# A transformer block on one core: where weight stores are issued, how weights are asked for ahead, and how buffers for gathered rows are cut

## The chip, the core and the metric

The kernel runs on one core of a Trainium2 chip. A core has five engines with queues of their own: TensorE (PE in the profile) multiplies matrices, VectorE (DVE) and ScalarE (ACT) do elementwise work and read the matmul results from PSUM, GpSimd (POOL) does elementwise work on SBUF and issues indirect copies, and SyncE (SP) only issues copies. Copies (DMAs) can be issued from the queues of SP, ScalarE and GpSimd; a queue runs its instructions in order, so an instruction that waits holds up all behind it. The metric is the device time of one execution in microseconds. Before the change it is 1752.19 us (median of three runs, 1750.74 to 1757.38).

## What is computed

A cross-attention step adds to `x` (4 x 512 x 512) a mixture of its own normalised rows; then comes a transformer layer with 16 causal heads of width 128 and a mixture of 16 experts, of which each token uses 6, beside a shared expert. Cut to what matters:

```
# cross-attention, per batch
x = x + layernorm(x) @ softmax((ctx Wq^T + bq) (ctx Wk^T + bk)^T)
# layer on h0 = layernorm(x)
h = rmsnorm(h0) * ln1;  q, k, v = h wq, h wk, h wv          # 16 heads of 128
x2 = h0 + softmax(causal(q k^T / sqrt(128))) v @ wo
t = rmsnorm(x2) * ln2
cw = top 6 of softmax(t gate^T), normalised
routed = sum over the 6 experts e: cw_e * (silu(t eg_e^T) * (t eu_e^T)) @ ed_e^T
shared = (silu(t sg^T) * (t su^T)) @ sd^T
out = x + x2 + routed + shared
```

All of it is in float32. The kernel keeps that precision by splitting each float32 operand into two float16 halves, high and low.

## The kernel before

**Split and product.** `split` (L72 to 74) turns a float32 tile into halves: ScalarE writes the high one (L73), VectorE the low one (L74). `mm3` (L80 to 88) multiplies two split operands with three matmuls per term (lines L83, L86, L87 of the profile). Transposes are made by DMAs on SP's queue (`flip`, L91).

**Order.** The program is written out straight and is handed to a planner that orders the instructions of each engine from a simulated timeline (`schedule_with_timeline_sim=True`) and sets the semaphores. `after(a, b)` only says that `a` comes behind `b` on the same engine's queue; `pin` keeps an instruction in program order. A tile from a pool with `bufs=n` can be filled again only when every reader of the tile n before it is through, DMAs that store it included.

**Stage 1, cross-attention (`xattn(b)`).** Batch 0 runs at the start, batch 1 soon behind it, batches 2 and 3 are spread over the attention loop. For each of four token tiles `t` the result `xv` (the new residual, L337) is stored to DRAM, `x1_d` (L339): from SP's queue for batch 0, from GpSimd's for the others. Then come the statistics on VectorE, a power on GpSimd (L347, which makes a reciprocal root), the normalised row `hd` or `x2` on GpSimd (L354), for batches 2 and 3 its store `hid_d` (L356), the split of `hh` and its transpose into `hT`.

**Stage 2, attention (the loop at L799, one head per step `n`, 64 in all).** A step multiplies `hT` with a head's `wqk` (`queries`) and every second step with `wv` (`values`), forms scores and softmax (`scores`, with the transpose of `pn` into `pt`), weighs the values of the head one step back (`attend`), and, when a group of two heads is through, multiplies with `wo` (`project`, L719 to 724) one step after its second head was weighed. A group is run for two batches in a row with the same weights.

`fetch` (L416 to 453) supplies weights. The first time a weight is wanted it is loaded as float32 into a staging tile `st` (L442, GpSimd's queue but for one; two staging tiles, shared with other loads of the loop), split, and the halves are stored to DRAM (`wqk_d`, `wv_d`, `wo_d`; L448, GpSimd's queue but for `wqk0`). Later the halves are loaded from there (L425, on ScalarE's queue); with `behind` given, that load is issued ahead of use, behind the instruction named. `wqk` and `wv` are asked for two steps ahead (L817 to 821), `wo` right after the group's second head was weighed, one step ahead of `project`:

```python
            attend(b, h)
            if h % HG == HG - 1:
                ready.append((b, h // HG))
                wo_of(b, h // HG, zz["ao"])
```

In steps 8 to 23 `pad_rows` (L498 to 502) copies 384 KB of zeros per step into the buffer of routed rows, from GpSimd's queue, each behind the weight store named `zz["pad"]`. `rest_step` (L541 to 549) reads `x1_d` back, adds, and stores `r_d`, all on GpSimd.

**Stage 3, shared expert and experts.** `gate_up` makes the shared expert's hidden activations in six chunks `ic`, three to a tile of `hs`, two such tiles (L741, L783, L875); `shared_down` (L768 to 781) multiplies them. Each of 16 experts runs in two halves (`gate_up_rows`, then `down_rows` with the store of `yt`, L1148). In the last experts rows of results are gathered back, 96 gathers of 128 rows in all (`gather`, L1194, GpSimd), and added with their weights on VectorE (L1203). Each gathered block takes a place in a ring: two tiles of three places, of the same tag as `hs`; an addition is put into the program once more than four gathered blocks are waiting (`lookahead`, `place`, `add`). After the experts the shared expert of the last batch runs, with the last gathers in tiles of `xin`.

Of the kernel before, what the change touches and what calls it, by code (L numbers as in the profile page):

```python
# [9 lines left out]
F16 = mybir.dt.float16  # L10
F32 = mybir.dt.float32
# [6 lines left out]
P = 128  # L18
# [37 lines left out]
def xattn_moe_block_kernel(ctx: ExitStack, tc: tile.TileContext, x, xT, ctxT, wqkx, bqk, ln1, ln2,  # L56
# [147 lines left out]
    def xattn(b):  # L204
# [127 lines left out]
        for t in range(NT):  # L332
            ps = bank("w", f"xm{b}_{t}")
            tl = slice(t * P, (t + 1) * P)
            xv = xt[:, t, :]
            zz["xm", b, t] = mm3(ps, [(lnp[:, c, tl], lnp[:, C + c, tl], ptp[:, c], ptp[:, C + c]) for c in range(C)])
            nc.vector.scalar_tensor_tensor(xv, ps, rs[:, t:t + 1], xv, ALU.mult, ALU.add)  # L337
            q = nc.gpsimd if b else nc.sync
            q.dma_start(x1_d[b][:, t, :], xv)  # L339
            st = asm.tile([P, 6], F32, name="st")  # L340
            nc.vector.bn_stats(st, xv)
            mv = asm.tile([P, 2], F32, name="mv")
            nc.vector.bn_aggr(mv, st)
            r2 = asm.tile([P, 2], F32, name="r2")
            nc.vector.tensor_scalar(r2[:, 0:1], mv[:, 1:2], 1e-5, None, ALU.add)
            nc.vector.tensor_scalar(r2[:, 1:2], mv[:, 1:2], 1.0 + 1e-6, 1e-11, ALU.mult, ALU.add)
            nc.gpsimd.tensor_tensor(r2, r2, mhalf[:, :2], ALU.pow)  # L347
            hu = tmp("hu", F32)
            nc.vector.scalar_tensor_tensor(hu, xv, mv[:, 0:1], ln1b, ALU.subtract, ALU.mult)
            yield  # L350
            nb = asm.tile([P, 1], F32, name="nb")
            nc.vector.scalar_tensor_tensor(nb, mv[:, 0:1], -1.0, r2[:, 0:1], ALU.mult, ALU.mult)
            hd = x2s[b][:, t] if b < 2 else tmp("hd", F32)
            nc.gpsimd.tensor_scalar(hd, xv, r2[:, 0:1], nb, ALU.mult, ALU.add)  # L354
            if b >= 2:
                q.dma_start(hid_d[b][:, t, :], hd)  # L356
            if stop == "A":
                nc.sync.dma_start(out[b, tl], hd)
            yield
            hh, hi, lo = pair(tmp("hh", F16))  # L360
            zz["hh", b] = split(hi, lo, hu, r2[:, 1:2])[1]
            zz["hT", b] = flip(hT[b][:, :, tl], hh)
            yield

# [51 lines left out]
    def fetch(b, g, pool, tag, n, src, scr, nm, behind=None):  # L416
        if behind and (nm not in seen or nm in soon):
            return
        if held.get(nm, (None,))[0] == (b, g):
            return None if behind else held.pop(nm)[1]  # L420
        w = soon.pop(nm, None)
        if w is None:
            w = pool.tile([P, 2, n], F16, tag=tag, name=f"{nm}_{b}")
            if nm in seen:
                ins = nc.scalar.dma_start(w.rearrange("p a n -> p (a n)"), scr)  # L425
                if behind:
                    after(ins, behind)
        if behind:
            soon[nm] = w
            return  # L430
        if (b, g) in partner:
            held[nm] = partner[b, g], w
        if nm in seen:
            return w
        seen.add(nm)
        first = nm in early_st
        if first:
            st_ = early_st[nm]
        else:
            st_ = stg.tile([P, 1024], F32, tag="st", name=f"{nm}_st")  # L440
            q = nc.sync if nm == "wqk1" else nc.gpsimd
            ins = q.dma_start(st_[:, :n], src)  # L442
            if nm == "wqk1":
                after(ins, zz["hT", 0])
        for j, ins in enumerate(split(w[:, 0], w[:, 1], st_[:, :n], WS)):
            if first:
                after(ins, zz["nb"] if j else zz["calm"][0])
        ins = (nc.sync if nm == "wqk0" else nc.gpsimd).dma_start(scr, w.rearrange("p a n -> p (a n)"))  # L448
        if nm != "wqk0":
            zz["pad"] = ins  # L450
        if nm == "wqk0":
            after(ins, zz["ptp", 0])
        return w

    pieces = []

# [278 lines left out]
    def gate_up(b, hid, tmp):  # L735
        shw = shx["w"]
        hs = []
        for ic in range(6):
            R = P if ic < 5 else SR
            if ic % 3 == 0:  # L740
                hs.append(hid().rearrange("p (i a s) -> p i a s", i=3, a=2))  # L741
            h = hs[-1][:, ic % 3]

            def proj(ps, a):
                o0 = ic * 8 * P + a * C * P
                zz["gu"] = mm3(ps, [(shw[:, 0, o0 + c * P:o0 + (c + 1) * P], shw[:, 1, o0 + c * P:o0 + (c + 1) * P],
                          h2T[b][:, c], h2T[b][:, C + c]) for c in range(C)])
# [20 lines left out]
    def shared_down(b, hs, last=False, tick=lambda src: None):  # L768
        sdw = shx["d"]
        acc = residual(b)  # L770
        for t in range(NT):
            tl = slice(t * P, (t + 1) * P)
            ps = bank("s", f"sy{b}_{t}")
            mm3(ps, [(hs[ic // 3][:, ic % 3, 0, tl], hs[ic // 3][:, ic % 3, 1, tl],
                      sdw[:, 0, ic * D:(ic + 1) * D], sdw[:, 1, ic * D:(ic + 1) * D]) for ic in range(5)], stop=False)
            nc.tensor.matmul(ps, hs[1][:, 2, 0, tl], sdw[:, 0, 5 * D:], start=False, stop=False)
            nc.tensor.matmul(ps, hs[1][:SR, 2, 1, tl], sdw[:SR, 0, 5 * D:], start=False, stop=True)
            zz["acc", b] = nc.vector.scalar_tensor_tensor(acc[:, t], ps, 1.0 / (GS * WS), acc[:, t], ALU.mult, ALU.add)
            if last:
                store(b * NT + t, acc[:, t])  # L780
            tick(acc[0:1, t, 0:1])

    early = gate_up(0, lambda: ht.tile([P, 2 * NT, S], F16, tag="pt", name="hs0").rearrange("p k s -> p (k s)")[:, :6 * S],  # L783
                    lambda: stg.tile([P, 1024], F32, tag="st", name="sg0")[:, :S])

    NH = B * H
# [10 lines left out]
    ready = []  # L797
    bring = iter([j for j in range(2, B) for _ in range(5 * NT + 1)])
    for n in range(NH + LAG + 1):  # L799
        if n < NH:  # L800
            b, h = heads[n]
            if b not in opened:
# [11 lines left out]
            for p in parts:  # L814
                for _ in p:
                    pass
            if n + HG < NH:  # L817
                b, h = heads[n + HG]
                wqk_of(b, h, zz["qk"])
                if h % HG == 0:  # L820
                    wv_of(b, h // HG, zz["qk"])
        m = n - LAG
        if n == NH:
            last_residual(B - 1)
        if n >= NH:
            for ic in range(3 * (n - NH), 3 * (n - NH) + 3):
                hs0 = next(early)
                if scat:
                    pace(hs0[ic // 3][0:1, ic % 3, 0, 0:1])
                    scatter(-(-len(scat) // (6 - ic)))  # L830
        if ready:
            b, g = ready.pop()
# [9 lines left out]
        if 0 <= m < NH:  # L842
            b, h = heads[m]
            attend(b, h)
            if h % HG == HG - 1:
                ready.append((b, h // HG))
                wo_of(b, h // HG, zz["ao"])
        if n in agenda and n < NH:
            b = agenda[n]
            if n + 1 in agenda:  # L850
# [21 lines left out]
    st2 = ctx.enter_context(tc.tile_pool(name="st2", bufs=2, side="right", reuse_waits="tile"))  # L872

    def up(b):
        return gate_up(b, lambda: st2.tile([P, 6 * S], F16, name="hs"), lambda: st2.tile([P, S], F32, name="sgt"))  # L875

    def drip(n, src):
        if scat:
# [34 lines left out]
        return o  # L913

    for ic, hs in zip((4, 5), ups):
        drip(2, hs[1][0:1, ic - 3, 0, 0:1])
    shared_down(1, hs, tick=lambda src: drip(2, src))
    residual(2)
    after(zz["exp"], zz["silu", 1, 1])
# [100 lines left out]
    seat(0)  # L1020
    nxt = ranked_weights(0)
    for ic, hs in enumerate(up(2)):
        drip(3, hs[ic // 3][0:1, ic % 3, 0, 0:1])
        if ic == 4:
            rows_in(0, 0)
            rows_in(0, 1)
# [192 lines left out]
        for _ in range(-(-len(todo) // left)):  # L1219
            gather()  # L1220

    lookahead(lambda: st2.tile([P, 3, D], F32, tag="hs", name="yg"), 3, 4)
    ring["steps"] = 1
    for e in range(E):
        wd = nxt
# [93 lines left out]
```

## Time and profile before

| what | value |
|---|---|
| time, median of three runs | 1752.19 us |
| the profiled execution | 1761.27 us |
| its span, first to last instruction | 1759.5 us |
| mean granted clock of TensorE | 0.993 |
| VectorE, ScalarE, GpSimd busy | 1114.4, 829.5, 459.2 us |
| weight stores on GpSimd (L448) | 31, of 0.53 to 0.54 us each (median) |
| residual stores on GpSimd (L339) | 12, of 0.55 us |
| weight loads on ScalarE's queue (L425) | 40, of 0.33 to 0.41 us |
| gathers (L1194) | 96, 1.13 us each on GpSimd |

Roughly, stage 1 of the first two batches runs to 88 us, attention to 1000 us, the experts from 1130 to 1710 us. Each row of a group in the profile has the line, engine, operation, the tiles written and read, the number of instructions, busy time, mean time of one, and the idle time of the engine in front of them with what ended it. A row of the timeline has start, duration, engine and operation, and in brackets the idle time before it and the instruction or DMA that ended it. In the list of waits a row gives who waited for whom: microseconds in total, times, the longest. A DMA's landing time is counted from its issue to its completion.

### The profile page before, as it was taken

The page shows a single profiled execution, that of the slowest core. Times are in us where ns is not written, and L with a number is a line of the kernel's source. Part 1 is how long each engine was busy: PE and PEld are TensorE (multiplying, and loading weights), DVE is VectorE, ACT ScalarE, POOL GpSimd, SP SyncE. Part 2 cuts the span into 40 slices and gives each one's busy share as a digit, 9 for nine tenths or more (in the row PEclk, how much of TensorE's full clock was granted, in tenths as well). Part 3 has the DMA queues.
Part 4 walks back from the last instruction along what each step waited for, and adds up shares of the span by engine and source line. Part 5 has one row for each costly group of instructions (what it writes and reads, how often), then busy time and mean ns, then how long its engine had stood idle before and what let it go on. Part 6 is the DMA issues. An engine that isn't in the chain of part 4 may idle for free. (4 is left out here: it accounts for less than half of the span.)

```text
span 1759.5 us, 27684 instructions
## 1 busy us (share of the span) xinstructions
PE 1711.6 (97%) x9919; PEld 933.2 (53%) x9919; DVE 1114.4 (63%) x2766; ACT 829.5 (47%) x1713; POOL 459.2 (26%) x574
## 2 busy tenths in 40 slices
PE   7899999999999999999999999999999999999998
PEld 3555556555555655556565544455555555554553
DVE  6778777778777777776667647544433444456755
ACT  4556655556544545554455522344544444443431
POOL 5524122140146243110003454300000000034654
PEclk9899999999999999999999999999999999999999
DMA  7696877566569787554447564755655456499766
GB/s 246 162 207 162 227 177 178 118 180 145 94 159 225 166 192 184 116 133 108 115 104 153 131 186 145 241 148 144 166 157 157 143 141 177 139 239 249 208 203 212
DMA packets 392212, 296.24 MB, mean 168 GB/s; under 512 B 334880, under 2 KB 335136, under 8 KB 391296
## 3 DMA queue, kind: packets, MB, share of 16 engines
q1 hardware_dynamic: 353360, 159.87, 40.3%
q0 software_dynamic: 32944, 113.53, 20.3%
q10 hardware_dynamic: 5760, 20.97, 4.4%
q8 instruction: 80, 1.31, 0.3%
q14 instruction: 68, 0.56, 0.1%
HBM read 124.81 MB, written 88.94 MB: 121 GB/s over the span
## 5 line engine op out<-in xcount | busy, mean ns | idle before, releaser
L1194 POOL DMA_INDIRECT yg<-y_d,yrc x96 | 108.7, 1132 | 509.1 <-PE u L87 425.7
L692 ACT ACTIVATE pe<-pe,bnm 128x128 f32<-128x128 f32 (+3 forms) x256 | 142.4, 557 | 188.1 <-DVE bnm L690 182.8
L83 PE MATMUL qk<-hT,wqk 128*128 128x512 f16 (+1 forms) x520 | 196.5, 378 | 4.0 <-DMA hT<-hh 3.7
L87 PE MATMUL qk<-hT,wqk 128*128 128x512 f16 (+1 forms) x520 | 196.5, 378 | 0.0
L86 PE MATMUL qk<-hT,wqk 128*128 128x512 f16 (+1 forms) x520 | 196.5, 378 | 0.0
L74 DVE SCALAR_TENSOR_TENSOR pn<-pe,brc,pn 128x128 f16<-128x128 f32 (+3 forms) x256 | 143.1, 574 | 20.4 <-ACT pn L73 17.7
L73 ACT ACTIVATE pn<-pe,brc 128x128 f16<-128x128 f32 (+3 forms) x256 | 133.0, 553 | 33.5 <-ACT pe L692 12.4
L690 DVE CUSTOM_DVE_ANT_0 pe<-sc,causal 128x128 f32<-128x128 f32 (+3 forms) x256 | 116.7, 486 | 40.9 <-PE sc L687 40.1
L83 PE MATMUL v<-wv,hT 128*128 128x256 f16 x512 | 139.9, 273 | 0.8 <-DMA hT<-hh 0.8
L86 PE MATMUL v<-wv,hT 128*128 128x256 f16 x512 | 139.9, 273 | 0.0
L87 PE MATMUL v<-wv,hT 128*128 128x256 f16 x512 | 139.8, 273 | 0.0
L83 PE MATMUL g<-xT,wt 128*128 128x384 f16 (+2 forms) x384 | 127.4, 332 | 0.0
L86 PE MATMUL g<-xT,wt 128*128 128x384 f16 (+2 forms) x384 | 127.3, 332 | 0.0
L87 PE MATMUL g<-xT,wt 128*128 128x384 f16 (+2 forms) x384 | 127.3, 332 | 0.0
L724 DVE SCALAR_TENSOR_TENSOR x<-wo,x 128x512 f32<-128x512 f32 x128 | 87.6, 688 | 45.9 <-PE wo L87 45.1
L1083 ACT ACTIVATE hT_e<-hf 128x384 f16<-128x384 f32 (+3 forms) x96 | 51.1, 532 | 136.7 <-DVE hf L1097 136.3
L83 PE MATMUL y<-dt,hT_e 128*128 128x512 f16 (+1 forms) x288 | 110.3, 383 | 0.0
L87 PE MATMUL y<-dt,hT_e 128*128 128x512 f16 (+1 forms) x288 | 109.5, 380 | 0.0
L86 PE MATMUL y<-dt,hT_e 128*128 128x512 f16 (+1 forms) x288 | 109.5, 380 | 0.0
L486 POOL DMA_INDIRECT xs_d<-h2p,slotu x96 | 97.7, 1018 | 28.4 <-issue 27.3
L83 PE MATMUL wo<-wo,ao 128*128 128x512 f16 x256 | 97.1, 379 | 5.3 <-DVE x L724 3.1
L74 DVE SCALAR_TENSOR_TENSOR qkt<-qk,qkt 128x512 f16<-128x512 f32 x128 | 87.7, 686 | 18.4 <-ACT qkt L73 13.9
(330 smaller groups left out, 4003.4 us busy)
## 6 DMA issues: line engine op xcount, KB each, us to landing
y_d<-yt SPq DMA_DIRECT2D x96, 256.0 KB, 2.6
est<-in_ew_dram SPq DMA_DIRECT2D x32, 704.0 KB, 6.5
est<-in_ed_dram SPq DMA_DIRECT2D x16, 768.0 KB, 4.4
wqk<-wqk_d ACTq DMA_DIRECT2D x20, 512.0 KB, 5.2
wqk_d<-wqk POOLq DMA_DIRECT2D x15, 512.0 KB, 3.1
wqk_st<-in_wqk_dram POOLq DMA_DIRECT2D x14, 512.0 KB, 5.9
xs_d<-causal POOLq DMA_DIRECT2D x16, 384.0 KB, 6.1
wv<-wv_d ACTq DMA_DIRECT2D x10, 512.0 KB, 5.4
```

Of the source, the lines that this page charges most:

```text
L73: return (nc.scalar.activation(hi, src, AF.Copy, scale=scale), nc.vector.scalar_tensor_tensor(lo, src, scale, hi, ALU.mult, ALU.subtract))
L74: nc.vector.scalar_tensor_tensor(lo, src, scale, hi, ALU.mult, ALU.subtract))
L83: ins = nc.tensor.matmul(o, lh, rh, start=start and j == 0, stop=False)
L86: nc.tensor.matmul(o, lh, rl, start=False, stop=False)
L87: ins = nc.tensor.matmul(o, ll, rh, start=False, stop=stop and j == n - 1)
L486: ins = nc.gpsimd.indirect_dma_start(out=xs_d, out_offset=bass.IndirectOffsetOnAxis(ap=slotu[:, tt, k:k + 1], axis=0), in_=h2ps[tt], in_of ...
L690: nc.vector.tensor_tensor_reduce(pe, ps[:, :w], causal[:, S - w:], -1.0, 3e38, ALU.add, ALU.min, nm)
L692: nc.scalar.activation(pe, pe, AF.Exp, bias=nm, scale=-1.0, accum_out=sm)
L724: nc.vector.scalar_tensor_tensor(x2[:, t, :], ps, 1.0 / (VS * WS), x2[:, t, :], ALU.mult, ALU.add)
L1083: nc.scalar.activation(hT[:R, ic, :w], hf, AF.Copy)
L1194: nc.gpsimd.indirect_dma_start(out=yg, out_offset=None, in_=src, in_offset=bass.IndirectOffsetOnAxis(ap=idx[:, tt, k:k + 1], axis=0))
```

## The change

Five things change; no arithmetic and no matmul does.

- **Weight stores.** `fetch` no longer stores the halves itself. It puts them on a list, `unsaved`, with the number of the step. `save(behind)` takes the oldest entry of an earlier step and issues its store on ScalarE's queue behind the instruction named. It is called twice per step: after the queries (behind the high half of `qkt`) and after `attend` (behind the high half of `ao`). `wqk0` stays on SP.
- **Residual stores.** For batches 1 to 3 `x1_d` is stored from ScalarE's queue, behind the high half of `hh`, no longer from GpSimd's.
- **Zero copies.** `zz["pad"]` is now the weight's load into staging, no longer its store.
- **`wo` ahead.** It is asked for in the step in which the group's second head makes its queries, behind `qkt`: one step earlier.
- **Places of one.** The chunks of `hs` and the gathered rows have tiles of one chunk or block, six of them, in the place of two tiles of three; an addition goes into the program once more than five blocks wait.

```diff
-            q = nc.gpsimd if b else nc.sync
-            q.dma_start(x1_d[b][:, t, :], xv)
+            if b == 0:
+                nc.sync.dma_start(x1_d[b][:, t, :], xv)
...
-            zz["hh", b] = split(hi, lo, hu, r2[:, 1:2])[1]
+            first, zz["hh", b] = split(hi, lo, hu, r2[:, 1:2])
+            if b:
+                after(nc.scalar.dma_start(x1_d[b][:, t, :], xv), first)
...
-            ins = q.dma_start(st_[:, :n], src)
+            zz["pad"] = ins = q.dma_start(st_[:, :n], src)
...
-        ins = (nc.sync if nm == "wqk0" else nc.gpsimd).dma_start(scr, w.rearrange("p a n -> p (a n)"))
-        if nm != "wqk0":
-            zz["pad"] = ins
         if nm == "wqk0":
-            after(ins, zz["ptp", 0])
+            after(nc.sync.dma_start(scr, w.rearrange("p a n -> p (a n)")), zz["ptp", 0])
+        else:
+            unsaved.append((scr, w, zz["n"]))
         return w
+
+    unsaved = []
+
+    def save(behind):
+        if unsaved and unsaved[0][2] < zz["n"]:
+            scr, w, _ = unsaved.pop(0)
+            after(nc.scalar.dma_start(scr, w.rearrange("p a n -> p (a n)")), behind)
...
-            if ic % 3 == 0:
-                hs.append(hid().rearrange("p (i a s) -> p i a s", i=3, a=2))
-            h = hs[-1][:, ic % 3]
+            h = hid(ic)
+            hs.append(h)
...
+            save(zz["qk"])
             if n + HG < NH:
                 b, h = heads[n + HG]
                 wqk_of(b, h, zz["qk"])
                 if h % HG == 0:
                     wv_of(b, h // HG, zz["qk"])
+            b, h = heads[n]
+            if h % HG == HG - 1:
+                wo_of(b, h // HG, zz["qk"])
...
             attend(b, h)
+            save(zz["ao"])
             if h % HG == HG - 1:
                 ready.append((b, h // HG))
-                wo_of(b, h // HG, zz["ao"])
...
-        return gate_up(b, lambda: st2.tile([P, 6 * S], F16, name="hs"), lambda: st2.tile([P, S], F32, name="sgt"))
+        return gate_up(b, lambda ic: st2.tile([P, 2, S], F16, name="hs", bufs=6), lambda: st2.tile([P, S], F32, name="sgt"))
...
-    lookahead(lambda: st2.tile([P, 3, D], F32, tag="hs", name="yg"), 3, 4)
+    lookahead(lambda: st2.tile([P, 1, D], F32, tag="hs", name="yg", bufs=6), 1, 5)
```

More of the change, by code (lines that the diff above doesn't have):

```diff
@@ L355, in xattn @@
             if b >= 2:
-                q.dma_start(hid_d[b][:, t, :], hd)
+                nc.gpsimd.dma_start(hid_d[b][:, t, :], hd)
             if stop == "A":
@@ L773, in shared_down @@
             ps = bank("s", f"sy{b}_{t}")
-            mm3(ps, [(hs[ic // 3][:, ic % 3, 0, tl], hs[ic // 3][:, ic % 3, 1, tl],
+            mm3(ps, [(hs[ic][:, 0, tl], hs[ic][:, 1, tl],
                       sdw[:, 0, ic * D:(ic + 1) * D], sdw[:, 1, ic * D:(ic + 1) * D]) for ic in range(5)], stop=False)
-            nc.tensor.matmul(ps, hs[1][:, 2, 0, tl], sdw[:, 0, 5 * D:], start=False, stop=False)
-            nc.tensor.matmul(ps, hs[1][:SR, 2, 1, tl], sdw[:SR, 0, 5 * D:], start=False, stop=True)
+            nc.tensor.matmul(ps, hs[5][:, 0, tl], sdw[:, 0, 5 * D:], start=False, stop=False)
+            nc.tensor.matmul(ps, hs[5][:SR, 1, tl], sdw[:SR, 0, 5 * D:], start=False, stop=True)
             zz["acc", b] = nc.vector.scalar_tensor_tensor(acc[:, t], ps, 1.0 / (GS * WS), acc[:, t], ALU.mult, ALU.add)
@@ L781, in shared_down, with early_hid @@
             tick(acc[0:1, t, 0:1])
-    early = gate_up(0, lambda: ht.tile([P, 2 * NT, S], F16, tag="pt", name="hs0").rearrange("p k s -> p (k s)")[:, :6 * S],
+    halves = []
+    def early_hid(ic):
+        if ic % 3 == 0:
+            t = ht.tile([P, 2 * NT, S], F16, tag="pt", name="hs0")
+            halves.append(t.rearrange("p (i a) s -> p i a s", a=2))
+        return halves[-1][:, ic % 3]
+    early = gate_up(0, early_hid,
                     lambda: stg.tile([P, 1024], F32, tag="st", name="sg0")[:, :S])
@@ L799, in xattn_moe_block_kernel @@
     for n in range(NH + LAG + 1):
+        zz["n"] = n
         if n < NH:
@@ L828, in xattn_moe_block_kernel @@
                 if scat:
-                    pace(hs0[ic // 3][0:1, ic % 3, 0, 0:1])
+                    pace(hs0[ic][0:1, 0, 0:1])
                     scatter(-(-len(scat) // (6 - ic)))
@@ L915, in xattn_moe_block_kernel @@
     for ic, hs in zip((4, 5), ups):
-        drip(2, hs[1][0:1, ic - 3, 0, 0:1])
+        drip(2, hs[ic][0:1, 0, 0:1])
     shared_down(1, hs, tick=lambda src: drip(2, src))
@@ L1022, in xattn_moe_block_kernel @@
     for ic, hs in enumerate(up(2)):
-        drip(3, hs[ic // 3][0:1, ic % 3, 0, 0:1])
+        drip(3, hs[ic][0:1, 0, 0:1])
         if ic == 4:
```

## The prediction

> **What bounds the kernel now.** I read the busy times first, then TensorE's timeline for its gaps, then what stood in front of each gap.
>
> ```profile
> span 1759.5 us, 27684 instructions
> PE 1711.6 (97%) x9919; PEld 933.2 (53%) x9919; DVE 1114.4 (63%) x2766; ACT 829.5 (47%) x1713; POOL 459.2 (26%) x574
> ```
>
> TensorE sets the time: it is idle for 1759.5 - 1711.6 = 47.9 us in all. The change touches no matmul, so it can only win from those 47.9 us and from stretches in which the granted clock is low. Of the gaps, 12.4 us lie before 53 us (input loads and the first batch's transposes, with stores that stay on SP) and about 7 us at the very end, behind the last matmul; the change does not reach those. About 28 us in the middle are left. TensorE's timeline, only the rows with a long gap (start, duration, operation, in brackets the idle time and what ended it):
>
> ```profile
> 79.06 0.58 PE L83 MATMUL xm<-ptp,lnp 128*128 128x512 f16 x1 [3.87 <-DMA ptp<-pn]
> ...
> 199.53 0.38 PE L83 MATMUL av<-pt,vt 128*128 128x512 f16 x1 [2.55 <-DMA pt<-pn]
> ...
> 510.50 0.38 PE L83 MATMUL wo<-wo,ao 128*128 128x512 f16 x1 [2.88 <-DVE x L724]
> ...
> 537.91 0.39 PE L83 MATMUL wo<-wo,ao 128*128 128x512 f16 x1 [2.27 <-DMA wo<-wo_d]
> ...
> 1624.05 0.32 PE L1106 MATMUL u<-xT,wb 128*128 128x384 f16 x1 [3.76 <-DVE hf L1097]
> ...
> 1644.37 0.32 PE L1106 MATMUL u<-xT,wb 128*128 128x384 f16 x1 [1.58 <-DVE hf L1097]
> ```
>
> Two gaps cost more than they show. After 79.06 eight matmuls take 3.34 us where eight at the usual 0.216 take 1.73, so 1.6 us more; after 1624.05 seven start 0.43 apart, 1.5 us more. After the 2.88 us gap at 510.50 the spacing is 0.21 at once. So a gap that shrinks from over 3.7 to under 2.9 us also gives back the slow matmuls. The six come to 16.9 us of idleness and 3.1 us of slow matmuls; seventeen gaps of 0.2 to 1.9 us make up the other 11.1.
>
> Why the gaps are there is read one engine further back. Ahead of 199.53, GpSimd's timeline:
>
> ```profile
> 183.65 0.55 POOL L448 DMA_DIRECT2D wqk_d<-wqk  x1 [6.87 <-DVE brc L694]
> 184.19 1.44 POOL L502 DMA_DIRECT2D xs_d<-causal  x2
> 185.34 0.83 POOL L442 DMA_DIRECT2D wqk_st<-in_wqk_dram  x1
> 185.99 0.73 POOL L448 DMA_DIRECT2D wo_d<-wo  x1
> 186.51 0.91 POOL L502 DMA_DIRECT2D xs_d<-causal  x1
> 187.09 0.88 POOL L442 DMA_DIRECT2D wv_st<-in_wv_dram  x1
> ```
>
> and ScalarE's and GpSimd's waits:
>
> ```profile
> ACT wv L73 <- DMA wv_st<-in_wv_dram: 10.8, 5, 3.9
> ...
> POOL yg L1194 <- DVE acc L1203: 55.7, 19, 7.9
> ```
>
> Three copies of 384 KB and a store of 512 KB are issued ahead of the load of `wv_st`; it lands after 10.6 us (median of such loads: 6.4), ScalarE stands 3.87 us at its split, the softmax behind it is late, and TensorE waits 2.55 us for the transposed `pt`. The store at 183.65 itself had waited 6.87 us with the loads behind it.
>
> **The change part by part.** Base: the profiled execution, 1761.27 us (span 1759.5 and 1.8 around it). The median shown is 1752.19, 9.1 lower; I take differences from the profile and subtract them from 1752.19.
>
> *Weight stores to ScalarE's queue (L448, 31 of them).* GpSimd loses 31 issues of 0.54 us and 148 us of standing in front of them. Less comes of it than it seems: a load two weights on needs the staging buffer that the same split frees. At 200.29 the store of `wv` goes after 12.32 us, and the load at 201.40 needs that very split. So loads are not issued much sooner; they only lose the 512 KB ahead of them. ScalarE gains 31 issues, and 12 from the residual (below): 43 x 0.327 us (row of the weight loads already on its queue) = 14.1 us. It is 56% busy from 88 to 410 us, and each store is held back one step, so its split is over and it should wait for nothing. The cover is ScalarE's idle time; where TensorE hangs on the softmax chain it is gone. That was four times before 410 us: 4 x 0.327 = 1.3 us lost. Between nothing and, if all 43 lie on the path, 14.1 us, I take 1.3.
>
> *Pad copies (L502) behind loads instead of stores.* They leave the place in front of the late load. Gap 199.53: between 0 and 2.55 gained. The load should be near its median, 4 us sooner, more than the 3.87 that ScalarE stood: I take 2.0, since ScalarE stands 29.6 us at such loads in all and some of it stays. Next late is the softmax itself.
>
> *Gap 79.06.* The last transposes of `ptp` there land after 6.9 us (median), against 5.3 over all sixteen, beside the stores issued at 67.04 and 70.12. Those two move a step on, and two earlier ones take partly their place. Bounds: 0.65 lost (two ScalarE issues on the chain) to 5.5 gained (3.87 + 1.6). I take 1.6 off the gap, and with it the slow matmuls: 3.2.
>
> *Residual stores (L339, 12) to ScalarE, behind the split of `hh`.* GpSimd stands 126 us before them, but its next instruction, the power of L347, waits for the same VectorE chain. Where `xv` is stored, ScalarE has just run an operation that depends on it, so nothing waits. Gap 510.50: GpSimd's L347 stood behind an addition (L548) that waited 3.80 us for a load of `x1t`, which landed after 4.9 us, median 3.6, with one such store issued right after it. 0 to 3.4 (with 0.54 at 513.09); the addition stays in front, so 0.5.
>
> *`wo` asked for one step earlier.* At 530.02 the load is issued, 7.9 us later it has landed. A step is some 14 us (64 heads between about 88 and 1000 us). Its buffer is free: two buffers, one used up every four steps. The 2.27 us go. If ScalarE is late by as much, nothing: 0 to 2.27; I take 2.27. The instruction itself is not new.
>
> *Places of one for gathered rows, and shared-expert buffers in six.* Same bytes, same 96 gathers. Before, the first gather of each three waits until three rows of an older tile are added; now each waits for one, six back. Ahead of 1644.37 GpSimd stood 6.49 us at that, the addition then 4.65 us for the gather, and `hf` behind it in VectorE's queue: 1.58 goes. Ahead of 1624.05 another chain decides: ScalarE stands 9.22 us at L1128 for a store `y_d<-yt`, while the DMA share is 1.04 from 1600 to 1620. Gathers that come sooner don't relieve that, and may add to it. Bounds for that gap: 3.8 lost (it doubles) to 5.3 gained; I take 0. The six places of `hs` come free within the same last token tile: 0.
>
> *Order remade.* The kernel is ordered from a simulated timeline, so everything around the edits may move. No row shows that; the seventeen small gaps, 11.1 us, bound it both ways. I take 0.
>
> The Trainium skill ("DMA: Bandwidth & Descriptors", section "Issuing engines are not separate DMA queues") speaks against the first part: DMAs of all engines run on the same sixteen engines, and spreading them saves only the sequencer's issue time. By it alone the store move is worth nothing on TensorE's path, and my sum would be without the 2.0 and the 3.2, 1749.1. The rows above make me keep them: what stood in front of the load was copies and a store in its own queue, not issue time.
>
> Sum: 2.27 + 2.0 + 3.2 + 0.5 + 1.58 - 1.3 = 8.25 us; 1752.19 - 8.25 = **1744**.
>
> **The rivals.**
>
> *Nothing but `wo` arrives.* Store and load wait for the same split, the pads collide elsewhere, a new small gap comes for each old one. For it: the two staging buffers (200.29 and 201.40). Against: the plain order of 184 to 187 us. 2.27 less some issue time: 1750, from 1746 to 1755.
>
> *Slower: stores beside transposes.* On ScalarE's queue the stores no longer line up with GpSimd's loads, so all three run at once, and SP's transposes of `pt` land later. Place: the softmax chain up to 410 us. Price: TensorE's eight waits for `pt` sum to 8.6 us, 1.08 each. It decides once over 16 of the 43 stores cost one such wait: 17 us, which eats the 8 and adds 9: 1761 and above; all 43 would be 46 us, less the 8: 1790. For it: from 88 to 120 us the DMA share is 1.12, and `pt` takes 8.1 us from 110 to 121, median 3.6. Against: the same bytes ran beside the same transposes before, and with forty loads on ScalarE's queue after 450 us TensorE waits only 3.1 us for `pt`.
>
> *Much faster.* Gaps hang together, and most of those named go, 1624.05 with its slow matmuls included: 2.27 + 2.55 + 5.5 + 3.4 + 6.9 = 20.6, and part of the small ones: 1727 to 1733.
>
> **How the numbers follow.** Forecast (1733 to 1750): 0.54. Nothing but `wo`: 0.24. Slower: 0.11. Much faster: 0.11. A difference under about 0.5%, 8.8 us, cannot be told from no change: the line lies at 1743.4, inside the forecast, and 1761. Of the forecast 0.33 lie below it (its lower side holds the greater part, since several terms were taken well under their upper ends), 0.21 above. Faster 0.33 + 0.11 = 0.44; same 0.21 + 0.24 = 0.45; slower 0.11. The range 1731 to 1756 leaves out most of the slower case and a part of the much faster.
>
> **What would show it.** TensorE's total idle time near 40 us, with the same 9919 matmuls. No wait for `wo_d` on TensorE. ScalarE's waits for `wv_st`, `wo_st`, `wqk_st` (29.6 us) clearly lower, and no idle time of ScalarE in front of stores. GpSimd's waits for the additions under the 55.7 us, and 1.58 at 1644 gone. I am wrong if TensorE's waits for `pt` rise above 8.6 us, if a new gap over 3 us with slow matmuls behind it appears, or if the gap before `u` at the last experts grows.

## The result and the profile after

The change makes the kernel slower: 1769.96 us (median of 16 runs, 1760.39 to 1779.44) against 1753.63 for the kernel before in the same comparison (16 runs, 1747.53 to 1764.14). The ratio is 1.0087, with a 95% interval of 1.0067 to 1.0107. The forecast was 1744, a gain.

The profiled execution after took 1779.36 us, 18.1 more than the one before; it lies high among its runs. Its span and TensorE's row:

```profile
span 1777.6 us, 27740 instructions
PE 1717.4 (97%) x9919; PEld 935.9 (53%) x9919; DVE 1116.6 (63%) x2766; ACT 828.5 (47%) x1711; POOL 451.8 (25%) x531
```

The matmuls are the same 9919. TensorE's idle time grew from 47.9 to 60.2 us, and its busy time by 5.8 us, though the work is the same: matmuls that follow a long gap run slower for a while (behind the gap at 176 us they start 0.43 us apart in place of 0.21). 12.3 + 5.8 = 18.1 us, the whole difference. TensorE's timeline after, from 60 us on, the rows with a gap of 1.9 us or more:

```profile
76.34 0.39 PE L83 MATMUL xm<-ptp,lnp 128*128 128x512 f16 x1 [1.98 <-DMA ptp<-pn]
...
176.26 0.58 PE L83 MATMUL av<-pt,vt 128*128 128x512 f16 x1 [5.64 <-DMA pt<-pn]
...
524.45 0.38 PE L83 MATMUL av<-pt,vt 128*128 128x512 f16 x1 [3.27 <-DMA pt<-pn]
...
597.05 0.58 PE L83 MATMUL av<-pt,vt 128*128 128x512 f16 x1 [5.05 <-DMA pt<-pn]
...
978.49 0.58 PE L83 MATMUL av<-pt,vt 128*128 128x512 f16 x1 [6.05 <-DMA pt<-pn]
...
1618.37 0.32 PE L1126 MATMUL u<-xT,wb 128*128 128x384 f16 x1 [2.51 <-DVE hf L1117]
...
1639.43 0.48 PE L1126 MATMUL u<-xT,wb 128*128 128x384 f16 x1 [4.01 <-DVE hf L1117]
...
1679.01 0.48 PE L1126 MATMUL u<-xT,wb 128*128 128x384 f16 x1 [3.13 <-DVE hf L1117]
```

Of the gaps that the prediction named, 3.87 us at 79 is 1.98, the 2.27 in front of `wo` is gone, and so are 2.88 at 510 and 1.58 at 1644; the 3.76 at 1624 is there as 4.01 at 1639 (the experts begin 12.5 us later). Others came instead: four in front of `av`, where TensorE waits for the transposed softmax `pt`, and two more in front of `u` in the last experts. A second profile of the same program (the run `after_again` below, span 1765.3) has the gaps near 515, 587 and 967 us again (2.30, 3.69 and 4.82 us), but not the one at 176 us. Its one gap before `u` of this size is 3.88 us. What one profile shows is therefore partly the execution and not the program, and the causes are sought with timed runs. The waits after:

```profile
POOL yg L1214 <- DVE acc L1223: 44.3, 19, 6.4
...
PE av L83 <- DMA pt<-pn: 26.3, 9, 6.0
...
PE u L1126 <- DVE hf L1117: 9.7, 3, 4.0
...
ACT wqk L73 <- DMA wqk_d<-wqk: 3.5, 2, 3.1
```

TensorE's waits for `pt` rose from 8.6 to 26.3 us (16.9 in the second profile), those for `hf` before `u` from 5.3 to 9.7 (4.1 in the second). So the three signs that the prediction gave for being wrong are all there in the first profile, and the first two in the second as well. GpSimd's waits for additions fell from 55.7 to 44.3 us, as predicted. The last row is new: ScalarE, about to split a `wqk`, waits for the *store* of an older `wqk`. No such row stands in the profile before. It is a small sum, and it leads to the one cause that could be followed.

### The profile page after: what moved, and what is told of

Its sections match the earlier page's. It is cut to its first block, busy times and chain, and to the rows that moved or that the text cites. A ratio compares the mean times of both kernels' runs of the same rounds, so it can differ in the third digit from the quotient of the medians.

```text
span 1777.6 us, 27740 instructions
## 1 busy us (share of the span) xinstructions
PE 1717.4 (97%) x9919; PEld 935.9 (53%) x9919; DVE 1116.6 (63%) x2766; ACT 828.5 (47%) x1711; POOL 451.8 (25%) x531
## 4 chain that ended last, share of the span: by engine, by line
PE 55%; DMA 4%; DVE 1%; ACT 1%; issue 0%; SPq 0%; POOL 0%; ACTq 0%
PE y L83 3%; PE y L86 3%; PE y L87 3%; PE g L86 3%; PE g L83 3%; PE g L87 3%; PE u L87 2%; PE u L83 2%; PE u L86 2%; PE qk L87 2%; PE qk L83 2%; PE qk L86 2%; DMA y_d<-yt 2%; PE u L1126 1%; PE u L1127 1%; PE wo L87 1%
## 5 line engine op out<-in xcount | busy, mean ns | idle before, releaser
L1214 POOL DMA_INDIRECT yg<-y_d,yrc x96 | 116.4, 1213 | 508.3 <-DVE hf L1117 436.0
L74 DVE SCALAR_TENSOR_TENSOR pn<-pe,brc,pn 128x128 f16<-128x128 f32 (+3 forms) x256 | 149.1, 591 | 25.5 <-ACT pn L73 22.0
L73 ACT ACTIVATE qkt<-qk 128x512 f16<-128x512 f32 x128 | 75.1, 587 | 75.4 <-PE qk L87 73.3
```

Of the source, the lines that this page charges most:

```text
L73: return (nc.scalar.activation(hi, src, AF.Copy, scale=scale), nc.vector.scalar_tensor_tensor(lo, src, scale, hi, ALU.mult, ALU.subtract))
L74: nc.vector.scalar_tensor_tensor(lo, src, scale, hi, ALU.mult, ALU.subtract))
L1214: nc.gpsimd.indirect_dma_start(out=yg, out_offset=None, in_=src, in_offset=bass.IndirectOffsetOnAxis(ap=idx[:, tt, k:k + 1], axis=0))
```

## The experiments

After the result there were three theories. **A**: the moved transfers cost, at their new places. **B**: the remade order costs. Compared as built, instruction by instruction, 2406 of the 9919 matmuls stand elsewhere than in the kernel before, all of them before about 1130 us; the experts' matmuls have not moved. **C**: the moves gain what was predicted, and something else hides it. All ratios are to the kernel before on the same chip, with 95% intervals.

### Each part alone

`only_store` has the hunks of the diff for the weight stores and the zero copies, `only_resid` that for `x1_d`, `only_wo` that for `wo`, `only_ring` those for the places of one:

```diff
 # only_store
-        ins = (nc.sync if nm == "wqk0" else nc.gpsimd).dma_start(scr, ...)
+            unsaved.append((scr, w, zz["n"]))        # and save() twice per step
 # only_resid
-            q.dma_start(x1_d[b][:, t, :], xv)
+                after(nc.scalar.dma_start(x1_d[b][:, t, :], xv), first)
 # only_wo
-                wo_of(b, h // HG, zz["ao"])
+                wo_of(b, h // HG, zz["qk"])
 # only_ring
-    lookahead(lambda: st2.tile([P, 3, D], F32, tag="hs", name="yg"), 3, 4)
+    lookahead(lambda: st2.tile([P, 1, D], F32, tag="hs", name="yg", bufs=6), 1, 5)
```

> The kernel before, with the places of one alone (shared-expert chunks and gathered rows). Theory A, gathers that run ahead crowd the stores of yt: slower by 4 to 8 us, the loss in the experts from 1590 us on, with ScalarE's wait for y_d<-yt above the 48.9 us of before. Theory B, the remade order of attention is the whole cause: this part changes nothing before 1000 us, so within 3 us of before. Theory C, as predicted: 1 to 5 us faster.

> The kernel before, with wo asked for one step earlier alone. Theory A, loads bunched on one queue make the transposes late: slower by 4 to 10 us, gaps of TensorE for pt between 450 and 1000 us, none of them before 450. Theory B, remade order: anything within 8 us either way, with gaps at places where no load is under way. Theory C, as predicted: 2 us faster, the wait of 2.27 us gone and no new one.

> The kernel before, with the weight stores on ScalarE's queue and the zero copies behind loads, alone. Theory A, the stores and copies collide with transposes or loads: slower by 5 to 10 us, the gaps before 420 us. Theory B, remade order: gaps also between 420 and 1000 us, where nothing of this part is left but the order. Theory C, as predicted: 4 us faster, the gap near 199 us gone.

> The kernel before, with the residual stores on ScalarE's queue alone. Theory A, the stores cost where they stand: 0 to 2 us, before 580 us. Theory B, remade order: up to 8 us either way, gaps at other places than the twelve stores. Theory C, as predicted: within 1 us.

Measured:

| part | ratio | interval | matmuls elsewhere |
|---|---|---|---|
| places of one | 1.0029 | 0.9997 to 1.0061 | 0 |
| `wo` earlier | 1.0114 | 1.0055 to 1.0173 | 1327 |
| weight stores, pads | 1.0050 | 1.0023 to 1.0078 | 2684 |
| residual stores | 1.0044 | 1.0010 to 1.0078 | 1046 |

No part gains. The row of `wo` rests on the fewest runs and has the widest interval. The parts add up to 2.4%, the whole loses 0.9%: they are not additive. And three of them move over a thousand matmuls, so a part alone doesn't tell A from B.

### Transfers and order exchanged

To tell them apart, a kernel can be held to another kernel's order: behind every instruction of an engine, the next one of the wanted order is queued with the same kind of edge that `after` sets, an order on the queue and no wait.

```diff
+    for key in order:                       # every instruction of the main block, in the wanted order
+        i = traced[key]
+        if i.engine in prev:
+            tc.add_manual_dep(i, prev[i.engine].name, NoSync, reason="order held")
+        prev[i.engine] = i
```

What the change itself moves is left out of `order` and finds its place by itself. In all kernels with "old order" matmuls and SyncE's instructions stand exactly as before.

> The whole change, with every matmul, every SyncE instruction and nearly everything else held to the places that the kernel before gives them; free are only the instructions that the change itself touches (the stores and splits of the attention weights, the residual stores, the gathered rows and their additions). The change as it stands moves 2406 of the 9919 matmuls to other places, all before about 1130 us. Theory A (the moved transfers themselves cost it: bunched on ScalarE's queue, they stretch transposes and loads that something waits for) expects a ratio to the kernel before of 1.006 to 1.012, as the change has. Theory B (the remade order costs it) expects 0.997 to 1.002. Theory C (the moves gain what was predicted once the order stays) expects 0.995 or less.

> The kernel before, with its stores and loads where they were, its matmuls and SyncE's instructions held to the order that the change got (2406 of 9919 matmuls elsewhere than in the kernel before; GpSimd is left free). Theory A (the transfers) expects 0.998 to 1.002, as nothing of the transfers' own places moves. Theory B (the order) expects 1.006 to 1.012. If both play, it and the kernel with the new code in the old order each lie near 1.004.

> The change unedited, beside the two kernels with exchanged orders on the same chip: all theories expect the ratio of its own comparison, 1.0067 to 1.0107. A ratio nearer to 1 here would say that the loss depends on the chip.

> The weight stores on ScalarE's queue alone, matmuls and SyncE's instructions held to the places of the kernel before; alone and with its own order this part took 1.0050 (1.0023 to 1.0078), with 2684 matmuls elsewhere. Theory A expects 1.003 to 1.008 again, theory B 0.997 to 1.002, theory C 0.998 or less (the pad loads no longer queued behind stores: 2.0 us predicted, 0.9989).

Measured: the change's transfers in the old order 1.0168 (1.0133 to 1.0203); the old transfers in the new order 1.0260 (1.0220 to 1.0301); the change itself 1.0089 (1.0052 to 1.0125), as the first time; the store part in the old order 1.0127 (1.0086 to 1.0168). Each mixture is worse than both kernels, so here an order fits the transfers that it was made for. And the change's own order is not needed for a loss: its transfers lose at least as much in the old one. Whether the own order takes part of it back (1.0168 without it, 1.0089 with it) is not settled: with more of the loads held, below, the old order gives 1.0102. What happens to an order without its transfers is read in TensorE's waits in the old code with the new order:

```profile
PE av L83 <- DMA pt<-pn: 18.4, 5, 6.9
...
PE wo L83 <- DMA wo<-wo_d: 11.2, 5, 4.6
```

Five waits for the projection weights, 11.2 us, against one of 2.3 us before: in this code the loads are asked for a step later than in the change, while the matmuls stand in the order that was made for earlier loads. That is a part of it: TensorE's idle time in this profile is 82.5 us, 34.6 more than before.

### A remade order without any moved transfer

Ten reductions that nothing reads make the planner lay out the order anew, though no transfer is moved. One kernel has them in the new order that comes of it, one in the old order (the price of the reductions), and a later one at other steps:

```diff
+        if n in (4, 10, 16, 22, 28, 34, 40, 46, 52, 58):    # other order: (8, 14, 20, 26, 32, 38, 44, 50, 56, 61)
+            pin(nc.vector.tensor_reduce(bsm.tile([P, NT], F32, name="rms")[:, :1], causal[:, :S - P], axis=AX.X, op=ALU.max))
```

> The kernel before with ten reductions of a constant 128x384 tile on VectorE, spread over the attention steps, that nothing reads (at most about 0.7 us each, by the reduction of line 310 that takes 677 ns for 512 columns; VectorE is idle 37% of the span). No transfer is moved, but the order is remade: 1777 of 9919 matmuls stand elsewhere. Theory A (the moved transfers cost it): ratio 0.998 to 1.002. Theory B (a remade order costs by itself, as the order of the kernel before happens to be a good one): 1.004 to 1.010. The two lie apart from 1.003 on.

> The same ten reductions with everything else held to the places of the kernel before: the price of the reductions themselves. Both theories: 0.999 to 1.002 (all ten on the path would be 7 us, 1.004).

> The ten idle reductions at other steps: again no transfer is moved, 1933 matmuls stand elsewhere than in the kernel before, 814 elsewhere than with the first idle work (1.0055). If a remade order costs in general, because the kernel before was tuned with its own: 1.003 to 1.009. If the first was an unlucky instance: 0.997 to 1.002.

Measured: 1.0055 (1.0025 to 1.0084) in the new order, 0.9985 (0.9958 to 1.0013) in the old one, 1.0000 (0.9968 to 1.0031) at the other steps. So laying out the order anew can cost 1.0055 / 0.9985 = 0.7%, some 12 us, with no transfer touched, or nothing. Theory B holds as a scatter of this size in two tries, not as a rule.

### Residual stores and reloads in the old order

The edits are those of `only_resid` and `only_wo`, the rest held to the old order; of `wo` only the ten reloads are earlier, since GpSimd's order, and with it the first loads, is held.

> The residual stores of blocks 1 to 3 on ScalarE's queue (12 stores), everything else held to the places of the kernel before. With its own order this part took 1.0044 (1.0010 to 1.0078), with 1046 matmuls elsewhere. Theory A: 1.002 to 1.008 again. Theory B: 0.998 to 1.002. If the order that the planner makes fits the moved stores, taking it away makes it worse: above 1.008.

> The reloads of the projection weights (ten, blocks 1 to 3) earlier, everything else held to the places of the kernel before; the first loads stay where they were, since GpSimd's order is held. With its own order, and with the first loads earlier too, this part took 1.0114 (1.0055 to 1.0173), with 1327 matmuls elsewhere. Theory A: 1.004 to 1.012. Theory B: 0.996 to 1.002, as the wait of 2.3 us for such a reload goes.

Measured: 1.0032 (1.0002 to 1.0063) and 1.0058 (1.0027 to 1.0088). The second fits theory A; the interval of the first reaches from no change into theory A. With the earlier reloads TensorE's wait of 2.3 us for `wo` is gone, as predicted, and the kernel is still slower; its profile (span 1762.3, idle 50.2 us) has new gaps in other places, 3.77 us for the routing at 644 us and 3.18 us at 967 us. Why they follow from ten loads one step earlier these runs don't show.

### Why the weight stores cost

The store part is the one that the runs follow furthest towards its cause. First two kernels that take its two halves apart, and the change without this part:

```diff
 # stores_at_once_old_order: ScalarE's queue, but right behind the split
+        after(nc.scalar.dma_start(scr, ...), high_half_of_the_split)
 # stores_late_gpsimd_old_order: put into the program a step later, but on GpSimd's queue
-            after(nc.scalar.dma_start(scr, ...), behind)
+            nc.gpsimd.dma_start(scr, ...)
 # without_store_part: the change, with the stores in fetch as before
-            unsaved.append((scr, w, zz["n"]))
+        ins = nc.gpsimd.dma_start(scr, ...)
```

> Weight stores on ScalarE's queue right behind the split, not a step later; GpSimd is freed of them as in the change, and the pads may follow the load. Everything but the 31 stores is held to the places of the kernel before. If the lateness costs (the weight's place is held until the late store has landed, and the next split into it waits): 0.998 to 1.003. If ScalarE's queue or the freed GpSimd costs: 1.008 to 1.013, as the late stores in the old order (1.0127).

> Weight stores a step later, as in the change, but still on GpSimd's queue; everything else held to the places of the kernel before but for the splits of the weights, which must wait for the stores. If the lateness costs: 1.008 to 1.013. If ScalarE's queue costs: 0.998 to 1.003.

> The change without its store part (weight stores on GpSimd at once, pads behind them), in its own order, with 2205 matmuls elsewhere. If the stores' transfers make the loss: 1.000 to 1.004. If a remade order makes most of it: 1.005 to 1.010, near the whole change's 1.0087.

Measured: at once on ScalarE's queue 0.9992 (0.9964 to 1.0020); later in the program on GpSimd's 1.0002 (0.9969 to 1.0035); the change without the store part 1.0083 (1.0051 to 1.0115). The first clears ScalarE's queue, and GpSimd freed of the stores. The second had an edit that did nothing: without an `after` the planner pulled the stores forward again, and in the trace the stores of `wqk` go out 0.3 to 2.0 us after their split, one after 5.1. It says nothing about lateness. It and the first have the zero copies behind loads, as in the change, and neither gains or loses measurably by it. The third says that the stores are not the only loss: without them the change's other parts, in their own order, lose as much.

Then the late stores on ScalarE's queue once more, with the loads of the weights held too (in `stores_old_order` the planner had put 12 of them elsewhere), and the whole change with those loads held:

```diff
 # stores_late_loads_held = only_store, new_code_loads_held = the change; both:
+    order: loads of wqk_st and wv_st kept in it (and of wo_st where wo is not moved)
```

> Weight stores a step later on ScalarE's queue, as in the change; matmuls, SyncE's instructions and the weights' loads on GpSimd held to the places of the kernel before, only the splits free. Against the kernel that left the loads free too (1.0127), 12 loads on GpSimd and 14 instructions on ScalarE stand elsewhere. If the stores themselves cost (late and on ScalarE's queue together): 1.008 to 1.014. If the loads placed anew cost it: 0.998 to 1.003.

> The whole change in the old order, with the loads of the first attention weights held as well (free are the moved stores, the splits, the projection weights, the gathered rows and their additions). With those loads free it took 1.0168. If the transfers of the change cost by themselves: 1.010 to 1.018. If it was the loads placed anew: what reloads and residual stores cost in the old order, 1.0058 and 1.0032, together 1.005 to 1.010. If the change gains once the order stays: below 1.

Measured: 1.0097 (1.0060 to 1.0133) and 1.0102 (1.0065 to 1.0140). The late stores alone cost as much as the whole change in the old order; with the loads left free it had been 1.0127 and 1.0168, so the loads placed anew may have added to it, though the intervals overlap.

So `stores_at_once_old_order` and `stores_late_loads_held` have the same matmul order and the same queue for the stores, and differ in when the stores go out, in what must wait for that, and in where the planner puts the splits among ScalarE's other work, which the late kernel leaves free. ScalarE's timeline from 58 to 102 us, only the rows with `wqk`, at once:

```profile
59.96 1.06 ACT L73 ACTIVATE wqk<-wqk_st 128x1024 f16<-128x1024 f32 x1
...
62.32 0.33 ACTq L449 DMA_DIRECT2D wqk_d<-wqk  x1
...
74.98 1.04 ACT L73 ACTIVATE wqk<-wqk_st 128x1024 f16<-128x1024 f32 x1
...
77.31 0.33 ACTq L449 DMA_DIRECT2D wqk_d<-wqk  x1
...
84.79 1.04 ACT L73 ACTIVATE wqk<-wqk_st 128x1024 f16<-128x1024 f32 x1
...
87.12 0.33 ACTq L449 DMA_DIRECT2D wqk_d<-wqk  x1
...
95.71 1.05 ACT L73 ACTIVATE wqk<-wqk_st 128x1024 f16<-128x1024 f32 x1
...
99.33 0.33 ACTq L449 DMA_DIRECT2D wqk_d<-wqk  x1
```

and late, followed by what TensorE does:

```profile
61.00 1.06 ACT L73 ACTIVATE wqk<-wqk_st 128x1024 f16<-128x1024 f32 x1
...
75.07 0.33 ACTq L459 DMA_DIRECT2D wqk_d<-wqk  x1
...
79.00 1.04 ACT L73 ACTIVATE wqk<-wqk_st 128x1024 f16<-128x1024 f32 x1
...
96.75 0.33 ACTq L459 DMA_DIRECT2D wqk_d<-wqk  x1
...
100.04 1.06 ACT L73 ACTIVATE wqk<-wqk_st 128x1024 f16<-128x1024 f32 x1 [2.71 <-DMA wqk_d<-wqk]
...
101.16 0.61 PE L83 MATMUL qk<-hT,wqk 128*128 128x512 f16 x1 [3.97 <-ACT wqk L73]
```

At once, four weights are split in these 44 us; late, three. There are two places for `wqk`, and a place can be filled again only when its store has landed. At 96.75 a store goes out, the next split waits 2.71 us until it has landed, and TensorE stands 3.97 us for that split; the matmuls behind it start about 0.42 us apart at first, half the usual pace. The kernel before and the one with stores at once have no such gap there; the three other kernels with late stores in the old order have it too (4.86 to 5.60 us, between 103 and 106 us). It goes on: the split frees the staging tile, so the next load on GpSimd is late as well (that of `wo_st` goes out at 102.7 us, against 92.9 at once).

In the change itself the same wait reaches ScalarE, but in neither of its two profiles TensorE by more than 0.2 us: no gap between 85 and 130 us is over 0.4 us. ScalarE's row in the first profile (3.35 us at 117 us in the second):

```profile
117.46 1.06 ACT L73 ACTIVATE wqk<-wqk_st 128x1024 f16<-128x1024 f32 x1 [3.14 <-DMA wqk_d<-wqk]
```

And the stores are later than the "one step" of the prediction. The step on the list is the one in whose text the weight is first used, and the planner runs load and split ahead of that. The store can't follow them: it is tied to `qkt` or `ao` of the step after the use. So its delay is the lead of the split and a step on top, and the steps of this stretch are long: the stores tied to steps 2 to 5 in the kernel with late stores go out at 75.07, 96.75, 112.31 and 137.29 us, some 21 us apart. In the kernel before the store floated with its split. From the end of a `wqk`'s split on VectorE to the issue of its store, read off the timelines:

| kernel | least | median of the first 13 | most |
|---|---|---|---|
| stores late, loads held | 18.5 us | 35.8 | 49.1 |
| the change | 15.4 us | 37.3 | 48.7 |
| stores at once | 0.02 us | 0.03 | 1.5 |

In the kernel before it is 0.3 to 4.5 us.

How much of the time comes of it can be followed in part. The three kernels before, at once and late run their matmuls in the same order, so the same matmul can be compared. Between the 400th and the 500th, where the gap of 3.97 us stands, the late kernel falls 5.9 us further behind the one with stores at once. By 400 us TensorE has begun 2193 matmuls before, 2201 at once and 2135 late, and the late kernel is 8.5 us behind the one at once. The one matmul `xixp` ahead of the experts starts at 1103.6, 1101.9 and 1120.0 us, so the lag has grown to 18.1 us. That is about the timed difference (1.0097 against 0.9992, some 18 us), but most of the second half arises between 450 and 615 us, when only the last weight stores go out (the last at 489 us), with gaps that kernels without late stores have too: TensorE waits 3.38 us for `pt` at 606 us in the late kernel, 3.39 at 599 us in `only_ring`. And single profiles scatter by as much: in `stores_late_gpsimd_old_order`, timed at 1.0002, `xixp` starts at 1114.6 us, and in the two profiles of the change at 1116.1 and 1104.7. So that late stores cost about 1% in the old order is measured; that it comes by way of the place which the store holds is seen in the traces for about a third of it (5.9 us), and for the rest it is not shown.

## Why the prediction was wrong

- **Weight stores: the step that failed, as far as the runs follow it.** The prediction put it so: "each store is held back one step, so its split is over and it should wait for nothing", and it priced ScalarE's issues alone, 1.3 us. ScalarE's issues indeed cost nothing that can be measured (at once on that queue 0.9992). But it asked only what the store waits for, not who waits for the store. The store is a reader of the weight's place. Held back, by 36 to 37 us at the median after its split and not by a step of 14, it makes two places act like fewer, and the next split, the next load and TensorE wait in turn. In the old order the part costs 1.0097, 17 us; in its own order 1.0050, 9 us. In the change as a whole only ScalarE's wait is seen, and without this part it still takes 1.0083, so this step alone does not make the loss.
- **Order remade, taken as 0.** The bounds of 11.1 us both ways were of the right size: one remade order without any moved transfer cost 0.7%, some 12 us, another nothing. The mistake was to let this not reach the chances: a loss of that size is larger than all the gains summed, and the range's upper end, 1756, has room for it only if every gain arrives.
- **`wo`, 2.27 us.** The wait went, as predicted, and the part is slower: 1.0114 alone, 1.0058 with only the reloads and the old order. The gain was read off one gap and nothing was set against it.
- **Gap 79.06, 3.2 us.** Right in kind: 3.87 became 1.98, with no slow matmuls behind it (1.78 in the second profile). So a gain that was there is contained in the loss. The reading behind it, that a gap under 2.9 us gives the slow matmuls back, does not always hold: in the second profile slow ones follow a gap of 2.30 us.
- **Pads, 2.0 us.** The gap they were charged with is not in the new profiles at its place, but in one of them a load with pads behind it is late:

```profile
164.44 0.53 POOL L444 DMA_DIRECT2D wqk_st<-in_wqk_dram  x1 [1.62 <-DVE wv L74]
164.96 1.45 POOL L510 DMA_DIRECT2D xs_d<-causal  x2
...
176.06 1.06 ACT L73 ACTIVATE wqk<-wqk_st 128x1024 f16<-128x1024 f32 x1 [8.37 <-DMA wqk_st<-in_wqk_dram]
```

  Two copies go out right behind the load, it lands after 11.6 us, ScalarE stands 8.37 us, TensorE 5.64. The second profile has the same three issues 0.2 us earlier and no such gap. And with stores at once ScalarE stands 7.21 us for the load of `wqk_st` issued at 164.69, TensorE 6.66, with no pad right behind that load. So it is not shown that the pads make this gap, and no gain of 2.0 us is shown either: 0.9992 and 1.0002 with pads behind loads, where 2.0 us is too small to tell. ScalarE's waits for first loads, 29.6 us before, are 34.6 after and 28.6 in the second profile, where they should have fallen clearly.
- **Residual stores, 0.5 us, and places of one, 1.58 us.** The first cost 0.3 to 0.4% instead. With the second the waits for additions fell as predicted, and the time stayed within what can be told from no change (1.0029, 0.9997 to 1.0061).
- **The rival on the slower side** had the sign right, with 0.11, and a mechanism that the runs do not bear out: it blamed stores on ScalarE's queue running beside the transposes, on the softmax chain up to 410 us. With the stores at once on that queue nothing is lost, and of the change's long waits for `pt` all but the one at 176 us lie behind 450 us. TensorE's waits for `pt` did rise, as it said. That stores which go out later meet other transposes than before, and cost something by that, was not tested apart from the place they hold. The Trainium skill ("DMA: Bandwidth & Descriptors", section "Issuing engines are not separate DMA queues") says that DMAs end up on the same 16 DMA engines whichever engine issued them, and that issuing from several saves issue time alone, usually small beside the transfer; the 0.9992 agrees.

What stays open: the four parts lose 2.4% one by one and 0.9% together, and without the store part the rest loses 0.8% all the same. In the old order the late stores alone cost what the whole change costs (1.0097 and 1.0102); in the change's own order their share can't be split off, since the other parts lose as much without them. The gaps for `pt` near 590 and 970 us, which both profiles of the change show, were not traced to one edit. In that first stretch the six transposes land late beside loads of 1.0 MB on ScalarE's queue, another 1.0 MB on SyncE's and four scatters; this was read, not tested. The DMA rows of the change from 572 to 598 us, with the median time to landing:

```profile
pt<-pn SPq DMA_TRANSPOSE x6, 8.9
xs_d<-h2p,slotu POOLq DMA_INDIRECT x4, 9.0
```

(3.6 us for `pt` over the whole of the kernel before).

## What to carry to other kernels

When a store is moved to where its issue is free, ask who fills its source next: a store that goes out later holds its buffer longer, and with two places the next fill may have to wait for it; count the delay from the moment the data is there, not from the step in the program, since a planner may run the producer ahead. Where a planner lays out the order anew, every edit can carry a scatter (here 0 and 0.7%, in two tries) that a sum of single gaps does not contain, and it belongs in the range and in the chances. To tell an edit's own effect from the remade order, hold the order and move the edit alone, and then look in the trace whether the edit happened.

## What the runs showed of the hardware that was not expected

The queue that issues 512 KB stores made no measurable difference at nearly the same moments and in the same order of matmuls (0.9992, 0.9964 to 1.0020, ScalarE's against GpSimd's). How long TensorE stood still does not alone decide whether the matmuls behind run slower: after gaps of 2.51 us (the change) and 2.55 and 2.88 us (before) they lost under 0.2 us against the usual spacing, after one of 2.30 us (second profile of the change) 1.67 us. The duration of the first matmul does not tell it either: after 3.27 and 3.69 us it took 0.38 us, but the next ones slowed down and lost 1.4 to 1.5 us, as after 5.05 us, where the first took 0.58. Two profiles of one program, with the same order, differed by 12.3 us in span (1777.6 and 1765.3), with mean granted clocks of 0.987 and 0.992.
